# The end of a bidirectional scan kernel: six pairs of units put in another order

## The chip, the cores and the metric

The kernel runs on one core of one Trainium2 chip. A core has a matrix engine (PE, TensorE), whose weight loads are listed apart as PEld, and four others: DVE (VectorE), ACT (ScalarE), POOL (GpSimd) and SP (SyncE), which here only issues DMA transfers. Each engine works through its own list of instructions in order and waits on semaphores for the others. The metric is the device time of one execution in microseconds (us), lower being better.

## The reference

The input is a batch of four images with 128 channels and 96 x 96 points. Each image is normalised in groups, read along rows and along columns, forward and backward (four directions), and each of these sequences goes through a gated convolution and a linear recurrence. The four results are fused by a 1x1 convolution and added to the input. Cut to what matters here:

```python
u, gate = split(grouped_1x1(seq, in_proj))
u  = depthwise_conv5(silu(u))
s, a, bb, cc = ssm_in(u), decay(u), tanh(u @ Wb), tanh(u @ Wc)
hst = scan(a, bb * s)                       # h = a*h + bb*s along the sequence
u  = u + ssm_out(cc * hst + d * s)          # the "state product"
u  = mix(u * sigmoid(gate))
y  = out_proj(u)                            # folded with mix and fuse into one matrix
out = x + sum over four directions of fuse(y)
```

## The kernel before

All weights behind the gate (mix, out_proj, fuse) are folded into one matrix `w_fin`, so what follows the gate is one product. A unit is a quarter (one residue of the position modulo R = 4) of a strip of 16 rows or columns in one direction; it has N = 384 positions. A *pair* is the two units of opposite directions (s = 0 and s = 1) that share the engines' instructions. There are 192 pairs, eight phases (image by orientation) of 24. `pair(t)` starts the front part of a pair and finishes the back part of the pair six earlier (LAG), so when the loop over 192 pairs has ended the back parts of six pairs are left, and `tail()` does them. Nothing but the order in which the lines of `tail()` are written sets the order on each engine: the schedule is by hand, and the semaphores follow from the data.

The back parts in the tail are called here by letters, by the names that the program gives their tiles: A = 7_4_2 and B = 7_4_3 (pairs 186 and 187, the last two of strip 4), and C, D, E, F = 7_5_0 to 7_5_3 (pairs 188 to 191, strip 5, the last of all). Z = 7_4_1 is the pair ahead of them, whose gating is already done when the tail begins. The back part of a pair has these steps:

- *Scan* (L702, DVE): the recurrence over a whole strip, for all its four pairs at once, in two halves. Only C to F still wait for theirs, the last scan of the kernel.
- *Outputs* (L708 and L709, on POOL unless told otherwise): cc times the state, plus the other term, in 64 partitions x 384. A copy (L711 on POOL or, as `z_copy`, L909 on ACT) brings the result to the other 64 partitions.
- *Seed* (`under`, L505, ACT): u of a unit is copied into two PSUM banks, so that the state product adds to it.
- *State product* (`out_of`, L497, PE): four matmuls of 32 partitions into the banks SSM + 2s and SSM + 2s + 1, that is 0 and 1 for s = 0, 2 and 3 for s = 1.
- *Gating* (L577, DVE; for F in halves, L964): (gate + 1) times the PSUM banks, into u.
- *Product* (`accumulate`, L134 under L729, PE): eight matmuls with `w_fin` into one bank of PSUM; one for each unit, called A0, A1, B0 and so on here by pair and s.
- *Addition* into `acc` (L752, L754): for s = 0 through a copy of the bank on ACT (`ys`, L735 or L737) and an addition on POOL, for s = 1 in the tail straight from PSUM on DVE. The last pair's products and additions are in halves of 192 positions (L974 to L991), and each of its four additions releases one output transfer on SP.

`gate_units(n)` (L911) writes, for each s, the gating of pair n and the seed of pair n + 1 in the same banks: the seed has to wait until that gating has read them. `finish(n)` (L919) issues both products of a pair, into the banks 4 and 5 or 6 and 7. `add()` (L924) does the oldest waiting DVE addition and sends finished lines.

In the tail before, the order of the state products, S, and the products on PE is: S(A), Z0, Z1, S(B), A0, A1, B0, B1, S(C), S(D), C0, C1, S(E), D0, D1, S(F), E0, E1, F in four halves. The scan halves lie apart on DVE, with B's gating between them (L934, L937, L938). C's outputs are DVE's and their copy POOL's (L939); those of D, E and F are all POOL's (L940, L943).

Of the kernel before, what the change touches and what calls it, by code (L numbers as in the profile page):

```python
# [45 lines left out]
ALU = mybir.AluOpType  # L46

P = 128
# [19 lines left out]
def conv_preact_kernel(  # L68
# [424 lines left out]

    def out_of(bi, s, j):
        z = tbs[bi]
        r = slice(64 * j + 32 * s, 64 * j + 32 * s + 32)
        nc.tensor.matmul(bank(SSM + 2 * s + j)[:, :N], w_so[r, bass.ts(j, P)], z[r, :],  # L497
                         start=bi not in seeded, stop=True, skip_group_check=True)
# [3 lines left out]
    def under(bi, s):  # L502

        seeded.add(bi)
        nc.scalar.copy(psum[:, SSM + 2 * s : SSM + 2 * s + 2, :N], us[bi][:, s])  # L505
# [60 lines left out]
    def gating(bi, s):  # L566
# [7 lines left out]
        pz = psum[:, SSM + 2 * s : SSM + 2 * s + 2, :N]  # L574
# [131 lines left out]
    def outputs(i, copy=nc.gpsimd.tensor_copy, engine=nc.gpsimd):  # L706
        ta, tb, p = scans[units[i]["step"]], tbs[i], units[i]["p"]
        engine.tensor_mul(ta[0:64, p, :], tb[64:P, :], ta[64:P, p, :])  # L708
        engine.tensor_add(tb[0:64, :], ta[0:64, p, :], tb[0:64, :])  # L709
        if copy:  # L710
            copy(tb[64:P, :], tb[0:64, :])  # L711
# [186 lines left out]
    def tail():  # L898
# [12 lines left out]
        def gate_units(n):  # L911
            for s in range(2):
                gating(2 * n, s)
                under(2 * n + 2, s)
                if s == 0 and n > first + 1:
                    z_copy(n + 1)
            waiting.extend(units[2 * n : 2 * n + 2])

        def finish(n):  # L919
            banks = (4, 5) if n % 2 else (6, 7)  # L920
            accumulate(waiting.pop(0), banks[0])()
            wait.append(accumulate(waiting.pop(0), banks[1], nc.vector, True))

        def add():  # L924
            if wait:
                wait.pop(0)()
# [5 lines left out]
        for bk in (4, 5):  # L932
            accumulate(waiting.pop(0), bk)()
        scan(NU // UB - 1, 0)  # L934
        scale_s(NU - 2)
        ssm_out(first + 1)
        gate_units(first + 1)  # L937
        scan(NU // UB - 1, 1)  # L938
        outputs(2 * first + 4, nc.gpsimd.tensor_copy, nc.vector)  # L939
        outputs(2 * first + 6, None)  # L940
        for bk in (6, 7):
            wait.append(accumulate(waiting.pop(0), bk, nc.vector, True))
        for n in range(first + 4, end):  # L943
            outputs(2 * n, None)
        finish(first + 1)
        add()
        add()
        ssm_out(first + 2)
        for n in range(first + 2, end - 1):
            gate_units(n)  # L950
            add()
            if n > first + 2:
                finish(n - 1)
# [3 lines left out]
        for s in range(2):  # L957
# [3 lines left out]
            for e in range(2):  # L961
                r = bass.ts(e, half)
                pz = psum[:, SSM + 2 * s : SSM + 2 * s + 2, r]
                nc.vector.scalar_tensor_tensor(v[:, :, r], g[:, :, r], 1.0, pz, ALU.add, ALU.mult)  # L964
        add()
        finish(end - 2)
        add()
        for s in range(2):
            bu = units[last + s]
            v = us[last][:, s]  # L970
            for e in range(2):
                r = bass.ts(e, half)
                py = bank(4 + 2 * s + e)
                for j in range(2):  # L974
                    for c in range(4):
                        mm(py, c, w_fin[:, bu["dir"], j, 32 * c : 32 * c + 32], v[:, j, r],
                           j == 0, j == 1)
                y = py[:, :half]
                lines = bu["st"] * LN + e * LN // 2
                if s:  # L980
                    lines = HH - lines - LN // 2
                    y = y[:, ::-1]
                part = acc[:, bass.ds(lines, LN // 2), R - 1 - bu["p"] if s else bu["p"], :]
                y = y.rearrange("p (h m) -> p h m", m=M)
                if s:
                    nc.vector.tensor_add(part, y, part)
                else:
# [190 lines left out]
```

## Time and profile before

Four executions took 1817.16, 1820.51, 1816.78 and 1817.36 us; the median is 1817.26. The profiled execution took 1817.16 us, and the span of its trace, from the first to the last instruction, is 1815.4 us.

| | busy us | share of the span |
|---|---|---|
| PE | 1791.1 | 99% |
| ACT | 1561.7 | 86% |
| DVE | 1446.1 | 80% |
| POOL | 1428.8 | 79% |

The tail takes the last 37 us. From the timeline of that stretch (us from the start of the span):

| step | start |
|---|---|
| S(A) on PE | 1778.65 |
| Z0, Z1 on PE | 1779.68, 1781.37 |
| first half of the last scan on DVE | 1781.55 |
| S(B) on PE | 1782.80 |
| B's gating on DVE | 1783.81 |
| A0, A1, B0, B1 on PE | 1784.18 |
| second half of the last scan on DVE | 1785.67 |
| C's outputs on DVE | 1787.60 |
| S(C) on PE | 1789.57 |
| S(D) on PE | 1793.07 |
| S(E) on PE | 1800.13 |
| S(F) on PE | 1803.70 |
| last product ends on PE | 1810.42 |
| the four last additions end on DVE | 1809.04, 1809.61, 1810.27, 1810.85 |

In the views that follow, the chain of waits gives start, length, what; the timeline adds the operation, the output and input, the count of instructions merged and, in brackets, the idle time ahead and what ended it; the table by stretches gives for each engine the busy time and the number of instructions, then PEclk, the share of full speed that TensorE's clock was granted. PE's rows count two records for each matmul. A busy PE is one with a matmul under way, at whatever clock.

### The profile page before, as it was taken

What the parts mean: (1) busy time and instruction counts of PE and PEld (TensorE: products, weight loads), DVE (VectorE), ACT (ScalarE), POOL (GpSimd) and SP (SyncE); (2) the same over time, 40 slices, a digit from 0 to 9 for tenths busy, and PEclk for the clock granted to TensorE, in tenths of its full rate; (3) what the DMA queues carried; (4) which work ended last, traced back from release to release, by engine and by line L of the source; (5) the groups of instructions that cost most, each with busy time, mean ns of one, the idle gap of its engine ahead of it and who ended that gap; (6) DMA issues with size and microseconds to landing.
All of it is one profiled execution on the core that took longest, in us unless ns stands there. A gap on an engine that the chain in (4) does not pass through costs nothing.

```text
span 1815.4 us, 56931 instructions
## 1 busy us (share of the span) xinstructions
PE 1791.1 (99%) x24074; PEld 645.9 (36%) x24074; DVE 1446.1 (80%) x1462; ACT 1561.7 (86%) x2748; POOL 1428.8 (79%) x1475
## 2 busy tenths in 40 slices
PE   7999999999999999999999999999999999999998
PEld 3333333333333333333333333333333333333333
DVE  6888878787888887877778888787877788778886
ACT  4888888988988888898888888889888888888974
POOL 3587888788778888788877888878877888887785
PEclk9999999999999999999999999999999999999998
DMA  8555463444975465334696456453476643635434
GB/s 247 177 188 180 148 201 102 161 144 156 315 241 183 158 195 174 118 140 138 222 295 227 141 178 211 120 172 116 155 245 217 227 148 129 198 100 180 149 123 157
DMA packets 148047, 321.17 MB, mean 177 GB/s; under 512 B 14160, under 2 KB 115920, under 8 KB 147792
## 3 DMA queue, kind: packets, MB, share of 16 engines
q1 hardware_dynamic: 147648, 317.48, 53.4%
q8 instruction: 190, 3.11, 0.7%
q14 instruction: 65, 0.53, 0.1%
q10 hardware_dynamic: 144, 0.04, 0.0%
HBM read 185.21 MB, written 132.25 MB: 175 GB/s over the span
## 4 chain that ended last, share of the span: by engine, by line
PE 94%; DVE 2%; DMA 2%; ACT 1%; issue 0%; POOL 0%; SPq 0%; DVEq 0%; ACTq 0%; POOLq 0%
PE psum L134 81%; PE psum L497 8%; PE psum L491 5%; DVE psum L630 1%; DMA x_in<-in_xs 1%; DMA xs<-in_xr 1%; DVE u L577 0%; DMA acc<-in_xr 0%; DVE u L630 0%; ACT psum L505 0%; ACT psum L628 0%; ACT sil L470 0%; ACT u L611 0%; DVE t L702 0%; SPq L296 0%
## 5 line engine op out<-in xcount | busy, mean ns | idle before, releaser
L630 DVE SCALAR_TENSOR_TENSOR psum<-sil,small,psum 128x768 f32<-128x768 f32 x576 | 589.0, 1022 | 28.2 <-ACT psum L628 3.4
L577 DVE SCALAR_TENSOR_TENSOR u<-gate,psum 128x768 f32<-128x768 f32 x376 | 349.7, 953 | 273.9 <-ACT u L609 122.3
L134 PE MATMUL psum<-u,w_fin 128*32 128x384 f32 x6176 | 552.1, 487 | 0.2 <-ACT t L673 0.2
L134 PE MATMUL psum<-u,main 128*32 128x384 f32 x6144 | 534.7, 489 | 1.2 <-DVE u L630 1.1
L754 POOL TENSOR_TENSOR acc<-ys,acc 128x384 f32<-128x384 f32 x374 | 410.9, 1120 | 32.8 <-ACT ys L735 10.1
L708 POOL TENSOR_TENSOR t<-t,t 64x384 f32<-64x384 f32 x191 | 236.8, 1240 | 154.3 <-DVE t L702 70.5
L134 PEld LDWEIGHTS psum<-u,w_fin 128*32 128x32 f32 x6176 | 189.5, 110 | 319.7 <-issue 218.3
L134 PEld LDWEIGHTS psum<-u,main 128*32 128x32 f32 x6144 | 182.3, 110 | 324.0 <-issue 196.5
L505 ACT COPY psum<-u 128x768 f32<-128x768 f32 x352 | 276.7, 799 | 22.7 <-DVE u L630 11.3
L134 PE MATMUL psum<-sil,band 128*32 128x384 f32 x3072 | 285.1, 488 | 0.0
L675 POOL TENSOR_SCALAR t<-tm 64x384 f32<-64x384 f32 x191 | 177.2, 927 | 117.3 <-ACT tm L667 98.3
L709 POOL TENSOR_TENSOR t<-t,t 64x384 f32<-64x384 f32 x191 | 247.0, 1293 | 15.0
L497 PE MATMUL psum<-t,main 32*128 32x384 f32 x1536 | 242.2, 515 | 3.3 <-ACT psum L505 2.6
L628 ACT ACTIVATE psum<-sil,small 128x768 f32<-128x768 f32 x191 | 173.2, 907 | 57.9 <-DVE u L577 49.7
L514 ACT ACTIVATE gate<-psum,bnorm 128x384 f32<-128x384 f32 x384 | 191.8, 581 | 27.1 <-PE psum L491 25.5
L676 POOL TENSOR_TENSOR t<-t,tm 64x384 f32<-64x384 f32 x192 | 195.1, 1016 | 15.3
L630 DVE SCALAR_TENSOR_TENSOR u<-sil,small,psum 128x768 f32<-128x768 f32 x192 | 194.9, 1015 | 7.8
L470 ACT ACTIVATE sil<-psum,bnorm 128x385 f32<-128x385 f32 x384 | 191.8, 584 | 4.0 <-PE psum L134 1.8
L134 PE MATMUL psum<-sil,less 64*32 64x384 f32 x3072 | 168.2, 495 | 0.0
L491 PE MATMUL psum<-x_in,wn 32*128 32x384 f32 x768 | 157.5, 527 | 0.4 <-ACT u L609 0.4
L134 PEld LDWEIGHTS psum<-sil,band 128*32 128x32 f32 x3072 | 90.9, 109 | 169.0 <-issue 94.8
L711 POOL COPY t<-t 64x384 f32<-64x384 f32 x188 | 137.0, 729 | 15.5 <-PE psum L134 3.6
(102 smaller groups left out, 1475.4 us busy)
## 6 DMA issues: line engine op xcount, KB each, us to landing
sil<-sil SPq DMA_DIRECT2D x128, 770.0 KB, 6.6
kept<-gate SPq DMA_DIRECT2D x80, 768.0 KB, 3.7
gate<-kept SPq DMA_DIRECT2D x76, 768.0 KB, 4.6
x_in<-in_xs SPq DMA_DIRECT2D x192, 96.2 KB, 2.5
out<-acc SPq DMA_DIRECT2D x48, 384.0 KB, 7.8
acc<-in_xr SPq DMA_DIRECT2D x39, 384.0 KB, 6.5
xs<-in_xr SPq DMA_DIRECT2D x72, 192.0 KB, 5.5
x_in<-in_xs SPq DMA_DIRECT2D x46, 192.5 KB, 3.4
```

The costliest lines, as they stand in the source:

```text
L134: nc.tensor.matmul(o[r, : rhs.shape[-1]], lhsT, rhs, start=start, stop=stop, skip_group_check=True)
L470: nc.scalar.activation(sils[step][:, s, j, g, :], bank(bk)[:, : N + 1], AF.Silu, bias=bn[:, 1:2] if j else bn[:, 4 + g : 5 + g],)
L491: nc.tensor.matmul(bank(to)[:, :N], stats[un["b"]][0][r, s, :], x_in[s][r, q, off : off + N], start=True, stop=True)
L497: nc.tensor.matmul(bank(SSM + 2 * s + j)[:, :N], w_so[r, bass.ts(j, P)], z[r, :], start=bi not in seeded, stop=True, skip_group_check=True)
L505: nc.scalar.copy(psum[:, SSM + 2 * s : SSM + 2 * s + 2, :N], us[bi][:, s])
L514: nc.scalar.activation(gv[:, s, j, :], bank(to[2 * s + j])[:, :N], AF.Tanh, bias=bn[:, 2 + j : 3 + j], scale=0.5,)
L577: nc.vector.scalar_tensor_tensor(v, g, 1.0, pz, ALU.add, ALU.mult)
L630: nc.vector.scalar_tensor_tensor(us[i][:, :, 1, :] if k == K - 1 else part, src, w_tap[:, k : k + 1], part, ALU.mult, ALU.add,)
L676: nc.gpsimd.tensor_mul(ta[0:64, p, :], tb[0:64, :], tm[0:64, :])
L708: engine.tensor_mul(ta[0:64, p, :], tb[64:P, :], ta[64:P, p, :])
L709: engine.tensor_add(tb[0:64, :], ta[0:64, p, :], tb[0:64, :])
L754: adder.tensor_add(part, y, part)
```

## The change

Only what lies behind the last pair is changed, by these edits:

- The last four pairs' state products take their banks in turn, (6, 7), (0, 1), (2, 3), one turn for each half pair: C in 6 and 0, D in 2 and 6, E in 0 and 2, F in 6 and 0 (the first bank of s = 0 and of s = 1). Products lie in banks 4 and 5 alone, one for s = 0 and one for s = 1.
- Both halves of the last scan stand together on DVE, ahead of B's gating. C's outputs are done on POOL in halves of 192 positions, each behind its half of the scan, and ahead of Z's two additions there. C's copy is ACT's `z_copy`.
- D's outputs go from POOL to DVE. POOL's order is C's outputs, Z's additions, E's outputs, the additions of A0 and B0, F's outputs, the additions of C0, D0, E0.
- On PE products and state products alternate: S(A), Z0, Z1, S(B), A0, A1, B0, S(C), B1, C0, S(D), C1, D0, S(E), D1, E0, S(F), then halves: E1, F0, F0, E1, F1, F1.
- `outputs` takes a range of positions, and the loop over the last products takes six halves rather than four, two of them E1's.

```diff
+    turning = (6, 0, 2)
+
+    def ssm(bi, s):
+        k = bi - NU + 8 + s
+        return turning[k % 3] if bi >= NU - 8 else SSM + 2 * s
...
-        nc.tensor.matmul(bank(SSM + 2 * s + j)[:, :N], w_so[r, bass.ts(j, P)], z[r, :],
+        nc.tensor.matmul(bank(ssm(bi, s) + j)[:, :N], w_so[r, bass.ts(j, P)], z[r, :],
...
-    def outputs(i, copy=nc.gpsimd.tensor_copy, engine=nc.gpsimd):
+    def outputs(i, copy=nc.gpsimd.tensor_copy, engine=nc.gpsimd, r=slice(0, N)):
...
             for s in range(2):
                 gating(2 * n, s)
                 under(2 * n + 2, s)
-                if s == 0 and n > first + 1:
-                    z_copy(n + 1)
-            waiting.extend(units[2 * n : 2 * n + 2])
-
-        def finish(n):
-            banks = (4, 5) if n % 2 else (6, 7)
-            accumulate(waiting.pop(0), banks[0])()
-            wait.append(accumulate(waiting.pop(0), banks[1], nc.vector, True))
+
+        def product(n, s, bk):
+            if s == 0:
+                accumulate(units[2 * n], bk)()
+            else:
+                wait.append(accumulate(units[2 * n + 1], bk, nc.vector, True))
...
         gate_units(first)
-        for bk in (4, 5):
-            accumulate(waiting.pop(0), bk)()
-        scan(NU // UB - 1, 0)
+        adds = [accumulate(waiting.pop(0), bk) for bk in (4, 5)]
         scale_s(NU - 2)
+        for part in range(2):
+            scan(NU // UB - 1, part)
+            outputs(2 * first + 4, None, r=bass.ts(part, N // 2))
         ssm_out(first + 1)
+        for held_add in adds:
+            held_add()
         gate_units(first + 1)
-        scan(NU // UB - 1, 1)
-        outputs(2 * first + 4, nc.gpsimd.tensor_copy, nc.vector)
-        outputs(2 * first + 6, None)
-        for bk in (6, 7):
-            wait.append(accumulate(waiting.pop(0), bk, nc.vector, True))
-        for n in range(first + 4, end):
-            outputs(2 * n, None)
-        finish(first + 1)
-        add()
+        outputs(2 * first + 6, None, nc.vector)
+        outputs(2 * first + 8, None)
+        product(first, 0, 4)
+        product(first, 1, 5)
+        z_copy(first + 2)
+        product(first + 1, 0, 4)
+        outputs(2 * first + 10, None)
         add()
         ssm_out(first + 2)
         for n in range(first + 2, end - 1):
             gate_units(n)
+            z_copy(n + 1)
+            product(n - 1, 1, 5)
             add()
-            if n > first + 2:
-                finish(n - 1)
+            product(n, 0, 4)
             ssm_out(n + 1)
...
-        add()
-        finish(end - 2)
-        add()
-        for s in range(2):
-            bu = units[last + s]
...
+        spots = iter((5, 4, 2, 3, 7, 6))
+        for i, s, e in ((-2, 1, 0), (-1, 0, 0), (-1, 0, 1), (-2, 1, 1), (-1, 1, 0), (-1, 1, 1)):
+            i += NU // 2
+            bu = units[2 * i + s]
+            r = bass.ts(e, half)
+            py = bank(next(spots))
+            for j in range(2):
+                for c in range(4):
+                    mm(py, c, w_fin[:, bu["dir"], j, 32 * c : 32 * c + 32], us[2 * i][:, s, j, r],
+                       j == 0, j == 1)
```

## The prediction

> **What bounds the kernel now.** I read the page first: PE is busy for 1791.1 of 1815.4 us and holds 94% of the chain of waits. Up to 1778.65 us both kernels issue the same instructions on every engine, so only the last 37 us can differ. There I read the chain of waits first (start, length, what):
>
> ```profile
> 1789.57 0.38 PE psum L497
> 1789.95 0.46 DVE acc L754
> 1790.41 0.72 issue
> 1791.13 0.97 DVE u L577
> 1792.10 0.02 issue
> 1792.12 0.81 ACT psum L505
> 1792.93 0.14 issue
> 1793.07 2.79 PE psum L497 x6
> 1795.86 4.34 PE psum L134 x32
> 1800.20 0.86 PE psum L497 x8
> 1801.06 2.72 PE psum L134 x32
> ```
>
> Behind S(C) PE has no product left to issue: the chain leaves it for C's gating and for the seed that must wait for that gating, and PE stands for 2.02 us (1791.05 to 1793.07). Then S(D) and two products take 2.79 and 4.34 us; a little later S(E) and two products take 0.86 and 2.72. The same work at two speeds: the table by stretches says why (length, busy us of the engines, then PEclk).
>
> ```profile
> 1791.10:1793.00 1.90, 0.00 (x0) 0.00 (x0) 1.87 (x3) 0.85 (x2) 1.75 (x3) 0.81 0.00 0
> 1794.00:1795.00 1.00, 1.00 (x6) 0.51 (x5) 0.00 (x0) 0.16 (x1) 1.00 (x1) 0.50 0.06 16
> 1798.00:1800.00 2.00, 2.00 (x20) 0.50 (x12) 0.00 (x0) 0.70 (x2) 1.32 (x2) 0.72 0.27 104
> ...
> 1788.87:1792.28 3.41, 2.16 (x20) 0.60 (x8) 2.69 (x5) 0.19 (x2) 2.54 (x3) 1.00 0.03 10
> 51.50:54.91 3.41, 2.73 (x64) 0.96 (x64) 3.34 (x5) 2.57 (x6) 1.30 (x2) 1.00 0.06 15
> 1792.28:1795.69 3.41, 2.62 (x8) 1.47 (x8) 1.64 (x3) 1.85 (x3) 3.18 (x4) 0.50 0.02 5
> 1795.69:1799.10 3.41, 3.41 (x26) 1.10 (x28) 1.32 (x2) 2.40 (x4) 2.86 (x3) 0.50 0.00 0
> ```
>
> The clock falls to 0.50 at 1792.28 (0.81 over the first stretch puts it there) and is back at 1799.10, 6.82 us later; it falls again at about 1812.74 (0.76 over 1812.5 to 1813.0), 13.64 later. Both are multiples of 3.41, so I read it as set at the end of such stretches: 2.16 busy of 3.41 lost the clock, 2.73 kept it, 2.62 did not win it back, 3.41 did.
>
> Third, whether DVE and POOL can work beside each other:
>
> ```profile
> 1748.63 2.81 DVE L702 TENSOR_TENSOR_SCAN t<-t,t 64x768 f32<-64x768 f32 x1
> 1748.63 1.20 POOL L709 TENSOR_TENSOR t<-t,t 64x384 f32<-64x384 f32 x1
> 1749.89 1.85 POOL L711 COPY t<-t 64x384 f32<-64x384 f32 x1
> ...
> 1781.55 1.81 DVE L702 TENSOR_TENSOR_SCAN t<-t,t 64x768 f32<-64x768 f32 x1
> ```
>
> Alone a scan half takes 1.81 us. Beside POOL it takes 2.81: it ends 1.61 after POOL's operation ends, and POOL's next one, a copy of 0.50 elsewhere, takes 1.85, to 0.30 behind the scan. So a DVE operation with two SBUF inputs and a POOL operation take turns. The gating, with one input in PSUM, takes 0.95 each beside POOL.
>
> Last, the end: the four output transfers (384 KB each) move 393 GB/s, about 1.0 us each, but their additions end only 1.81 us apart. So they queue, and the end follows the first of these additions (1809.04), 6.36 us behind it.
>
> **The change, step by step.** Prices: a product 1.35 (four in 5.37), a state product 0.85 to the next product and 1.05 to the first gating (1766.82 to 1767.88), two gatings 0.97 and 1.82, a seed 0.80, a `ys` 0.58, a z_copy 0.51, a half product 0.67 (E's two whole products and F's four halves take 5.39 together).
>
> *Scan halves and C's outputs.* The first half stays at 1781.55 to 1783.36. The second now starts at 1783.39, ends at 1785.22, 2.35 earlier. POOL is released a few hundredths behind DVE's own start (0.08 at 1688.56) and so waits for it. Its half-size operations are in no trace: the nearest rows are 1.20 (64x384) and, from below, 0.11 for POOL's smallest memset; halving the part that grows gives 0.65, bounds 0.55 and 1.20. Four of them, the first partly spent waiting: 1785.22 to 1787.75. Against that, DVE did C's outputs in 1.79 and POOL copied in 0.50 (to 1790.08). So C's result is 2.3 earlier. B's gating moves from 1783.81 to 1785.25; what waits for it is the seed of C's second half (bank 0) at 1786.24 to 1787.04; behind that in ACT's queue stands the ys of A0, to 1787.56, which frees bank 4 for B0. PE, done with A1 at 1786.88, waits 0.72 there: the first price of the order.
>
> *D's outputs on DVE* start at 1787.1, while POOL does C's last half and Z's additions (about 1.0 each). By the turns above: POOL to 1787.75, DVE's multiplication to 1788.50, one addition of Z to 1789.35, DVE's addition to 1790.10; 3.0 for what is 1.79 alone, bounds 1.8 and 4.2. Queued behind on DVE are A1's addition (to 1790.65) and C's gating.
>
> *PE.* B0 1787.60 to 1788.95, S(C) to 1789.80 (its copy is done at 1788.3, both seeds at 1787.04). B1 needs bank 5, free when A1 is added: PE waits 0.90, the second price. B1 1790.70, C0 1792.05 (C's gating 1790.67 to 1791.64), S(D) 1793.40. That is 0.33 later than before. From here each pair is S, product, product with nothing between: ACT has the seeds ready, because the banks turn (the bank of D's second seed, 6, is last read by C's first gating, a whole step earlier), and the z_copy ends 2.8 to 3.3 after S begins, ahead of the next S at 3.55. So S(E) 1796.95, S(F) 1800.50: 3.2 earlier than before. Of the 7.06 between S(D) and S(E), half speed and seed waits were 3.5.
>
> *POOL behind it:* Z's second addition to 1790.95, E's outputs to 1793.4, A0 and B0 added to 1795.4, F's outputs to 1797.8. F's copy is wanted by ACT at 1799.75: 1.95 of cover. B's four output transfers leave SP at about 1795.4, not 1798.65, and are through by 1799.5, before the last four. Halving E1 adds no matmul time (two of 0.67); it fills PE while F is gated.
>
> *The end.* F's gating 1801.55, four times 0.49, to 1803.50; E1's half addition 0.37, then F0's 0.43: first of the last four at 1804.30 against 1809.04. From S(F) that is 3.80 instead of 5.34. PE ends at 1805.4, the last addition at 1805.9, before 1810.85. Sum: 0.33 - 3.51 = -3.2 at S(F), -1.5 behind it, **-4.7 us**. The span becomes 1810.7; with the 1.76 outside the span the profiled execution's 1817.16 becomes 1812.5, and the median, 0.10 above, 1812.6. I say 1812.5.
>
> Bounds: half operations at 1.20 delay C's copy by 2.2, of which 0.65 is covered: +1.6. POOL ahead of the second scan half: +0.65. D's outputs between 1.8 and 4.2: -0.7 to +1.2. Together some 1811.3 to 1814.7, not all at once.
>
> **A rule against the trace.** The row comes first: a stretch of 3.41 us with 2.16 busy, and no idle time above 2.02, lost the clock. The Trainium skill, TensorE: Matmul & The Clock Gate, Part 1, says that the clock halves after at least one idle window of about 3.4 us, and its table warns of gaps above some 3 us. By the page no gap of the changed kernel comes near and the sum stands. By the row, 0.72 + 0.90 of waiting within 3.9 us could leave a stretch as little as 2.2 busy, and the time would be that of the first rival.
>
> **The rivals.** *The clock still falls* at one of the two new waits. For: 2.2 busy at the worst phase against 2.16 that lost it. Against: at the phase of this trace the stretches hold 2.7 and 2.5, near the 2.73 that kept it, and behind 1790.7 PE is continuous, so one or two stretches bring it back. Price: half of 3.41 or 6.82, 1.7 to 3.4: 1814.2 to 1815.9.
>
> *POOL and DVE in turns cost more than I give*: the half operations at their upper bound, or D's outputs losing every turn. For: no row of them. Price 1.0 to 2.5: 1813.5 to 1815.0.
>
> *Slower: the half clock stays.* Place: from 1792.28 on. At half speed S and two products last 7.1; if the state products, 32 partitions deep, count as less than busy, stretches may fall short again and again. It decides from three stretches on (5.1 us lost against 4.7 gained); four cost 6.8: 1819.3. Against: the full stretch 1795.69 to 1799.10 did restore it.
>
> *It does not act as said*: the two scan halves adjacent, yet C's state product hardly moves (0.6), since B0 now stands ahead of it. That is in my sum; if POOL loses fewer turns the gain is 5.5: 1811.8.
>
> **How the numbers follow.** Forecast with its near variants, 1811.5 to 1813.4: 0.60. Clock falls for one or two stretches: 0.20. Costlier turns: 0.11. Half clock stays, slower: 0.09. The range 1810.8 to 1816.0 takes in all but the last and some of the second. About 0.2%, 3.6 us, is what a measurement of this kernel can tell, so faster means below 1813.6: 0.60 and a little of the third, 0.62. Same takes the second and most of the third, 0.29; slower 0.09.
>
> **What would show it.** Right: PEclk 1.00 through to the end; S(D), S(E), S(F) 3.5 apart; waits of PE under 1 us, one before B0 and one before B1; POOL's first half operation stretched to the end of the second scan half; D's two operations on DVE lengthened; first of the last additions near 1804.3. Wrong: any 0.50 before that; a gap ahead of S(F) for F's copy; S(C) later than 1790.5.

## The result, and the profile after

The changed kernel took 1813.69 us (median of 33 executions, 1812.67 to 1817.91) against 1816.60 for the kernel before in the same sessions (53 executions, 1814.69 to 1820.51). The ratio is 0.9985, with a 95% interval of 0.9980 to 0.9990: 2.9 us faster, not 4.7. The profiled execution took 1814.49 us, its span is 1812.7, and the lines of the code are up by 7 (L709 is the scan, L715 and L716 the outputs, L761 the addition, L504 the state product).

The whole kernel is too coarse to see the difference in: S(A), the first step of the tail, stands at 1778.65 in the trace of before and at 1777.27 in that of after, though both kernels issue the same work up to there; in the kernels shown further on it stands between 1778.0 and 1780.3. So stretches that begin at S(A) are compared from here on. From S(A) to the end of the first of the last four additions it was 30.4 us before; the prediction made it 25.65; this trace shows 29.0. PE in this trace, with S(A), B0, B1 and C0 together, and S(F):

```profile
1777.27 1.10 PE L504 MATMUL psum<-t,main 32*128 32x384 f32 x8
...
1786.73 1.50 PE L134 MATMUL psum<-u,w_fin 128*32 128x384 f32 x16 [1.16 <-ACT ys L742]
...
1791.25 4.38 PE L134 MATMUL psum<-u,w_fin 128*32 128x384 f32 x32 [2.16 <-DVE acc L761]
...
1802.75 0.93 PE L504 MATMUL psum<-t,main 32*128 32x384 f32 x8
```

The loss against the prediction lies mostly in one place. The chain of waits (start, length, what) in the part that answers to the chain of before:

```profile
1784.38 1.83 DVE u L584 x2
...
1786.23 2.84 DVE t L715
1789.07 0.02 issue
1789.09 0.04 DVE t L716
...
1789.34 1.31 issue
1790.65 0.55 DVE acc L761
1791.20 0.04 issue
1791.25 4.38 PE psum L134 x32
1795.62 0.91 PE psum L504 x8
1796.53 2.72 PE psum L134 x32
1799.25 0.86 PE psum L504 x8
```

Read it upwards from S(D), the 0.91 at 1795.62. B1 and C0, the 4.38 ahead of it, began only when A1 had been added (0.55), since that frees B1's bank. A1's addition stood on DVE behind D's two outputs, and these took from 1786.23 to 1790.7, the second of them in the piece called "issue": it was under way, and the profile names nothing that it waited for. Also, B1 and C0 took 4.38, while the next two products took 2.72. The table by stretches (length, busy us of PE, PEld, DVE, ACT, POOL with the count, then PEclk, DMA share, GB/s), laid along the grid of 3.41 us on which the clock changes here (it falls at 1792.29 and is back at 1795.70), says why:

```profile
1785.46:1788.88 3.42, 2.26 (x28) 0.73 (x24) 3.39 (x2) 2.31 (x5) 3.26 (x5) 1.00 0.54 217
1788.88:1792.29 3.41, 1.25 (x20) 0.47 (x20) 3.38 (x5) 0.91 (x2) 3.33 (x3) 1.00 0.00 0
1792.29:1795.70 3.41, 3.41 (x28) 0.91 (x20) 1.18 (x2) 1.11 (x2) 3.25 (x4) 0.50 0.37 141
1795.70:1799.11 3.41, 3.41 (x40) 1.13 (x40) 2.29 (x3) 2.59 (x4) 1.50 (x2) 1.00 0.84 325
```

The wait of 1.16 before B0 left a stretch with 2.26 busy, which kept the clock; the longer wait before B1 left one with 1.25, and the clock was halved for the next, though PE was busy in all of it. The full stretch brought it back, once, where the kernel before lost it for 6.82. This is the price of the first rival, at its lower end.

What DVE and POOL did meanwhile, and DVE at the end, from the timeline (start, length, engine, line):

```profile
1782.01 2.34 DVE L709 TENSOR_TENSOR_SCAN t<-t 64x768 f32<-64x768 f32 x1
1782.06 0.69 POOL L715 TENSOR_TENSOR t<-t,t 64x192 f32<-64x192 f32 x1 [2.66 <-DVE t L709]
1782.82 2.02 POOL L716 TENSOR_TENSOR t<-t,t 64x192 f32<-64x192 f32 x1
...
1785.70 0.67 POOL L716 TENSOR_TENSOR t<-t,t 64x192 f32<-64x192 f32 x1
...
1786.23 2.83 DVE L715 TENSOR_TENSOR t<-t,t 64x384 f32<-64x384 f32 x1
1786.34 1.95 POOL L761 TENSOR_TENSOR acc<-ys,acc 128x384 f32<-128x384 f32 x2
...
1788.38 1.74 POOL L715 TENSOR_TENSOR t<-t,t 64x384 f32<-64x384 f32 x1
...
1789.09 1.63 DVE L716 TENSOR_TENSOR t<-t,t 64x384 f32<-64x384 f32 x1
...
1805.61 0.35 DVE L989 TENSOR_TENSOR acc<-psum,acc 128x192 f32<-128x192 f32 x1
1805.87 0.73 DVE L991 SCALAR_TENSOR_TENSOR acc<-psum,b_fin,acc 128x192 f32<-128x192 f32 x2
```

Twice POOL wins. Its first half operation, issued 0.05 behind the second scan half, takes 0.69, the length of an undisturbed one, and the scan half takes 2.34 instead of 1.81. Later DVE issues D's multiplication 0.14 before C's last half operation ends on POOL, and both of Z's additions (1.95 together, which is undisturbed) still pass it; POOL's next operation, E's multiplication, is the first that waits for DVE. What such a multiplication takes undisturbed shows in the kernel before, where DVE did C's outputs while POOL stood idle:

```profile
1787.60 0.90 DVE L708 TENSOR_TENSOR t<-t,t 64x384 f32<-64x384 f32 x1
```

Behind S(D) the trace is as predicted. State products start at 1795.55, 1799.18 and 1802.75, 3.6 apart. The rows at 1805.61 and 1805.87 are E1's first half addition and F0's two: the first of F0's ends some 3.5 us after S(F) begins, and the clock is 1.00 up to the last product.

This trace is not the median execution. Of the executions of the changed kernel whose clock is listed, 24 show a mean granted clock of 1.000 and a median of 1813.4 us, eight show 0.999 and 1814.7, among them the profiled one, and two show 0.998 (1817.1 and 1817.9). A whole stretch of 3.41 us at half clock takes 0.0009 off the mean, so by this record the 24 lost none. Half of a stretch, 1.7 us, on top of the 1.4 that the tail of this trace gained (30.4 to 29.0), makes 3.1, near the 2.9 of the medians. The mean alone doesn't say where a clock was lost, so this is worked out and not shown.

### The profile page after: what moved, and what is told of

It reads as the page before. It is cut to its first block, busy times and chain, and to the rows that moved or that the text cites. A ratio compares the mean times of both kernels' runs of the same rounds, so it can differ in the third digit from the quotient of the medians.

```text
span 1812.7 us, 56969 instructions
## 1 busy us (share of the span) xinstructions
PE 1788.8 (99%) x24090; PEld 645.2 (36%) x24090; DVE 1448.5 (80%) x1462; ACT 1562.6 (86%) x2750; POOL 1431.6 (79%) x1477
## 4 chain that ended last, share of the span: by engine, by line
PE 94%; DVE 3%; ACT 1%; DMA 1%; issue 0%; SPq 0%; POOL 0%; DVEq 0%; ACTq 0%; POOLq 0%
PE psum L134 81%; PE psum L504 8%; PE psum L491 5%; DVE psum L637 1%; DMA xs<-in_xr 1%; DMA acc<-in_xr 0%; DVE u L584 0%; DVE bn L298 0%; DVE u L637 0%; ACT psum L635 0%; ACT psum L512 0%; ACT u L618 0%; ACT sil L470 0%; DVE t L715 0%; DVE t L709 0%
## 5 line engine op out<-in xcount | busy, mean ns | idle before, releaser
L134 PE MATMUL psum<-u,w_fin 128*32 128x384 f32 (+1 forms) x6192 | 552.7, 486 | 3.5 <-DVE acc L761 2.2
L761 POOL TENSOR_TENSOR acc<-ys,acc 128x384 f32<-128x384 f32 x375 | 411.8, 1119 | 28.0 <-ACT ys L744 8.5
L715 POOL TENSOR_TENSOR t<-t,t 64x384 f32<-64x384 f32 (+1 forms) x192 | 237.3, 1236 | 156.7 <-DVE t L709 73.1
L716 POOL TENSOR_TENSOR t<-t,t 64x384 f32<-64x384 f32 (+1 forms) x192 | 248.6, 1295 | 15.1
L504 PE MATMUL psum<-t,main 32*128 32x384 f32 x1536 | 239.4, 513 | 1.3 <-ACT psum L512 0.6
```

Of the source, the lines that this page charges most:

```text
L134: nc.tensor.matmul(o[r, : rhs.shape[-1]], lhsT, rhs, start=start, stop=stop, skip_group_check=True)
L504: nc.tensor.matmul(bank(ssm(bi, s) + j)[:, :N], w_so[r, bass.ts(j, P)], z[r, :], start=bi not in seeded, stop=True, skip_group_check=True)
L715: engine.tensor_mul(ta[0:64, p, r], tb[64:P, r], ta[64:P, p, r])
L716: engine.tensor_add(tb[0:64, r], ta[0:64, p, r], tb[0:64, r])
L761: adder.tensor_add(part, y, part)
```

## The experiments

Ratios are against the kernel before on the same chip in the same session, with a 95% interval; the traces, one of each kernel, are compared from S(A) to S(F), which is 25.05 us before, 25.48 after, and 21.85 in the prediction's sum.

**Is the gain the clock?** The kernel before, with nine matmuls that compute nothing needed, into unused columns, where PE stood for 2.02 us:

```diff
+        def warm(n):
+            for _ in range(n):
+                nc.tensor.matmul(psum[:, 4, 384:512], ident, ident, start=True, stop=True,
+                                 skip_group_check=True)
...
         add()
         add()
         ssm_out(first + 2)
+        warm(9)
```

> The kernel before, with nine 128x128 matmuls on PE between S(C) and S(D), into columns that nothing reads; they only fill the 2.02 us in which PE stood. Theory 1 (most of what the change gains is the clock that the kernel before lost there): PEclk stays 1.00 to the end, S(D) to S(E) falls from 7.06 to about 4.1 us, the kernel is about 2.9 us faster than before (0.9984), as much as the whole change. Rival (the gain comes from the order; the clock is a by-product): S(D) to S(E) falls by no more than 1 us, since DVE and ACT set that stretch, and the ratio is 0.9995 or nearer to 1.

The ratio was 0.9986 [0.9976, 0.9996], 1816.04 us against 1818.90. The timeline of PE (the fillers are at L931):

```profile
1790.17 1.49 PE L497 MATMUL psum<-t,main 32*128 32x384 f32 x8
1791.59 2.27 PE L931 MATMUL psum<-ident 128*128 128x128 f32 x18
1793.80 1.94 PE L497 MATMUL psum<-t,main 32*128 32x384 f32 x8
1795.66 2.79 PE L134 MATMUL psum<-u,w_fin 128*32 128x384 f32 x32
1798.38 0.93 PE L497 MATMUL psum<-t,main 32*128 32x384 f32 x8
```

S(D) to S(E), the first two L497 behind the fillers, is 4.58 us instead of 7.06, C's products take 2.79 instead of 4.41, and from S(A) to S(F) it is 22.70. No wait of the order is removed. The other executions agree: nine of the twelve show a mean clock of 0.999 or 1.000, and of the 23 of the kernel before three do. So keeping the clock alone is worth as much as the whole change turned out to be.

**What is left with the clock kept in both?** The changed kernel with five such matmuls before B0 and nine before B1:

```diff
         z_copy(first + 2)
+        warm(5, 6)
         product(first + 1, 0, 4)
         outputs(2 * first + 10, None)
         add()
         ssm_out(first + 2)
+        warm(9, 4)
         for n in range(first + 2, end - 1):
```

`warm` takes how many and the bank in whose unused columns they are written.

> The changed kernel, with five such matmuls ahead of B0 and nine ahead of B1, in the 1.16 and 2.16 us in which PE stands there. Theory 1 (the clock still falls in a part of the executions, and this costs 1.7 us each time): all executions read a clock of 1.000 in the tail, the median falls by about 0.5 us against the changed kernel (0.9982 against before), and its slower executions go. Rival (the spread of the changed kernel's executions is something else): no difference in median or spread.

The ratio is 0.9981 [0.9971, 0.9991], 1815.45 us against the same 1818.90. From S(A) to S(F) 23.92, and behind S(F) the first addition ends 3.5 later, so 27.4 in all against 28.05 of the kernel before with fillers (22.70 and 5.35): the order by itself gains about 0.6 in these traces, and the ratios, whose intervals overlap, don't contradict that. Against the changed kernel's own 0.9985 the ratio isn't distinguishable either; the traces differ by 1.6, the half of one stretch. That every execution would keep its clock was not borne out: seven of twelve show 1.000, two 0.999 and three 0.996 to 0.998, and where those lost it no trace says.

**Is it D's outputs?** Back to POOL, as before the change:

```diff
-        outputs(2 * first + 6, None, nc.vector)
+        outputs(2 * first + 6, None)
```

> The changed kernel with D's outputs on POOL, behind Z's two additions and ahead of E's outputs, instead of on DVE. Theory 2 (on DVE they lose their turns to POOL: 4.49 us from issue to end where 1.79 is the work, and A1's addition, C's gating and B1 wait behind them): PE's wait of 2.16 us ahead of B1 is gone, the clock does not fall, S(C) to S(D) goes from 7.4 to about 3.6 us, and the kernel is 2.0 to 3.5 us faster than the changed one (about 0.997 against before). Rival (POOL is the bound, which is why D went to DVE): D's copy comes too late, a wait of 1 us or more moves ahead of S(D), S(E) or S(F), and the time is that of the changed kernel or longer.

The ratio is 0.9964 [0.9951, 0.9977], 1812.61 us against 1818.90: 6.3 us faster than the kernel before. PE:

```profile
1788.59 1.50 PE L134 MATMUL psum<-u,w_fin 128*32 128x384 f32 x16 [1.15 <-ACT ys L742]
1790.02 0.93 PE L504 MATMUL psum<-t,main 32*128 32x384 f32 x8
1790.87 2.79 PE L134 MATMUL psum<-u,w_fin 128*32 128x384 f32 x32
1793.59 0.93 PE L504 MATMUL psum<-t,main 32*128 32x384 f32 x8
```

The wait before B0 is the same 1.15, that before B1 is gone, B1 and C0 run at full speed, and from S(A) to S(F) it is 21.62, 3.9 less than in the changed kernel's trace. Of this 2.16 is the wait and 1.6 the half clock that followed it in this execution. By the ratios, 0.9985 and 0.9964 with intervals that don't overlap, though from different sessions, the edit that moved work to DVE cost 3.8: in the order of what the whole change gained. With this version the first of the last additions ends 25.1 behind S(A), against 28.05 in the kernel before with fillers, so without that edit the order brings some 2.9 beyond the clock.

**Or only its place beside Z's additions?** D's outputs stay on DVE, but Z's two additions go behind E's outputs on POOL:

```diff
-        for held_add in adds:
-            held_add()
         gate_units(first + 1)
         outputs(2 * first + 6, None, nc.vector)
         outputs(2 * first + 8, None)
+        for held_add in adds:
+            held_add()
```

> The changed kernel with Z's two additions on POOL behind E's outputs instead of ahead of them; D's outputs stay on DVE. Theory 2a (DVE loses the port for as long as POOL's operations follow one another with no wait on POOL's own result, as Z's two additions do; E's outputs wait for one another and let DVE in): D's outputs take 2.5 to 3.0 us from issue to end instead of 4.49, PE's wait ahead of B1 falls from 2.16 to about 0.5 us, and the kernel is 1.5 to 2.5 us faster than the changed one. Rival 2b (DVE gives way to any POOL operation that is ready): D's outputs still take over 4 us, ended by E's outputs, and the time is unchanged.

The ratio is 0.9966 [0.9955, 0.9978], 1813.34 us. DVE:

```profile
1788.81 0.87 DVE L715 TENSOR_TENSOR t<-t,t 64x384 f32<-64x384 f32 x1
1789.71 1.69 DVE L716 TENSOR_TENSOR t<-t,t 64x384 f32<-64x384 f32 x1
```

The pair takes 2.59 from first to last instead of 4.49, the wait before B1 is 0.26, and S(A) to S(F) is 21.95. The ratio can't be told from that of the version before it. So DVE was not the wrong engine; beside Z's additions was the wrong place.

**What are the scan halves together worth?** On the kernel with D's outputs on POOL, B's gating goes back between the halves:

```diff
-        for part in range(2):
-            scan(NU // UB - 1, part)
-            outputs(2 * first + 4, None, r=bass.ts(part, N // 2))
+        scan(NU // UB - 1, 0)
+        outputs(2 * first + 4, None, r=bass.ts(0, N // 2))
         ssm_out(first + 1)
+        gate_units(first + 1)
+        scan(NU // UB - 1, 1)
+        outputs(2 * first + 4, None, r=bass.ts(1, N // 2))
         for held_add in adds:
             held_add()
-        gate_units(first + 1)
```

> The kernel with D's outputs on POOL, one part of the change undone: B's gating stands again between the scan halves, and Z's two additions stand behind both of C's half outputs as they did. Theory 3 (the adjacent scan halves bring nothing by themselves: what C's result gains, B's gating loses, and B0's bank with it): PE's wait of 1.15 us ahead of B0 falls below 0.3 us and a wait of 1 us or so appears ahead of S(C) instead; the time is within 0.5 us of the kernel with D's outputs on POOL (0.996 to 0.9967 against before). Rival (adjacent halves are worth the 2.35 us by which the second half ends earlier): 1.5 us or more slower than that kernel.

The ratio is 0.9975 [0.9965, 0.9984], 1814.12 us against 1819.18. The wait before B0 is gone, since B's gating and the seed behind it are early; in its place PE waits for C's and D's results on POOL:

```profile
1789.39 1.46 PE L504 MATMUL psum<-t,main 32*128 32x384 f32 x8 [0.80 <-POOL t L716]
1790.79 2.79 PE L134 MATMUL psum<-u,w_fin 128*32 128x384 f32 x32
1793.89 1.46 PE L504 MATMUL psum<-t,main 32*128 32x384 f32 x8 [0.32 <-POOL t L716]
```

S(A) to S(F) is 22.58, 0.96 more than with the halves together: between the two expectations. The halves together bring about 1 us, and that is net of the wait before B0, which they make. This rests on the two traces; the intervals of the ratios, 0.9975 and 0.9964, overlap.

**What are the turning banks worth?** On the same kernel the last pairs' state products stay in banks 0 to 3 (and the last halves take banks that are then free):

```diff
-        return turning[k % 3] if bi >= NU - 8 else SSM + 2 * s
+        return SSM + 2 * s
...
-        spots = iter((5, 4, 2, 3, 7, 6))
+        spots = iter((5, 4, 6, 7, 0, 1))
```

> The kernel with D's outputs on POOL, another part undone: the state products keep their banks 0 to 3, so each seed waits for the gating of its own half, and F's halves use the banks 6, 7, 0, 1. Theory 4 (the turning banks are what lets the next state product follow two products directly): PE waits 0.5 to 0.8 us ahead of S(D), S(E) and S(F), 3.57 us from one to the next become 4.1 to 4.4, and the kernel is 1.5 to 2.4 us slower than with D's outputs on POOL. Rival (two products cover the seeds in either bank): no difference.

The ratio is 0.9994 [0.9985, 1.0003], 1816.92 us: nothing is left that can be told from the kernel before.

```profile
1790.63 1.50 PE L134 MATMUL psum<-u,w_fin 128*32 128x384 f32 x16 [2.02 <-ACT ys L742]
...
1795.63 1.58 PE L504 MATMUL psum<-t,main 32*128 32x384 f32 x8
1797.14 2.79 PE L134 MATMUL psum<-u,w_fin 128*32 128x384 f32 x32
1799.86 1.54 PE L504 MATMUL psum<-t,main 32*128 32x384 f32 x8
```

From S(D) on state products take 1.54 to 1.58 instead of 0.93 and stand 4.2 apart, as the banks of their seeds are read by a gating until shortly before; and the wait before B0 is longer by 0.87. S(A) to S(F) is 23.75, 2.1 more.

This trace also bears on the clock. PE stood for 2.02 us, as long as in the kernel before, and the clock stayed at 1.00. It falls at 1812.73, after the last product; counted back from there in steps of 3.41, the grid puts this row around the wait:

```profile
1788.83:1792.25 3.42, 1.62 (x20) 0.61 (x24) 0.87 (x2) 2.25 (x5) 3.34 (x4) 1.00 0.34 135
```

So 1.62 busy kept the clock here, where 2.16 lost it in the kernel before. Busy time alone is then not what decides. The two differ in what PE did: of the 2.16, 1.48 was a state product, 32 partitions deep, and 0.68 a product; of the 1.62, 0.19 was a state product and the rest a product. Whether a state product counts for less was not tested.

**A faster version.** The seeds of C wait for B's gating, and A0's `ys` stands behind them on ACT; that is the 1.15 before B0. So, on the kernel with D's outputs on POOL, A0's product and its `ys` are issued ahead of B's gating, its addition follows on POOL behind E's outputs, and B0 is added straight from PSUM by DVE:

```diff
-        for held_add in adds:
-            held_add()
+        adds.append(accumulate(units[2 * first], 4))
         gate_units(first + 1)
         outputs(2 * first + 6, None)
+        for held_add in adds[:2]:
+            held_add()
         outputs(2 * first + 8, None)
-        product(first, 0, 4)
+        adds[2]()
+        outputs(2 * first + 10, None)
         product(first, 1, 5)
         z_copy(first + 2)
-        product(first + 1, 0, 4)
-        outputs(2 * first + 10, None)
+        wait.append(accumulate(units[2 * first + 2], 4, nc.vector, True))
+        add()
         add()
```

> The kernel with D's outputs on POOL, and besides: A0's copy out of its bank on ACT goes ahead of C's seeds, B0 is added by DVE straight from PSUM, and POOL does D, Z, E, A0, F in this order. If PE's 1.15 us ahead of B0 are nothing but ACT's order (A0's copy behind a seed that waits for B's gating), they fall below 0.3 us, S(C) begins 0.9 to 1.3 us earlier after S(A), and the kernel is 0.9 to 1.3 us faster than with D's outputs on POOL (0.9955 to 0.996 against before). Rival (POOL's result for C is as late as the bank): the wait moves ahead of S(C), and the gain is under 0.3 us.

PE has no wait between S(B) and S(F), and S(A) to S(F) is 20.46, 1.16 less, as expected. The time was 1811.60 (1809.67 to 1817.96) and the ratio 0.9965 [0.9951, 0.9978], which isn't distinguishable from the version that it was made from; 1 us is within the intervals.

**The last product in halves.** The version with D's outputs on POOL, with E1 whole ahead of F's halves:

```diff
+        product(end - 2, 1, 5)
+        add()
-        spots = iter((5, 4, 2, 3, 7, 6))
-        for i, s, e in ((-2, 1, 0), (-1, 0, 0), (-1, 0, 1), (-2, 1, 1), (-1, 1, 0), (-1, 1, 1)):
+        spots = iter((4, 2, 7, 6))
+        for i, s, e in ((-1, 0, 0), (-1, 0, 1), (-1, 1, 0), (-1, 1, 1)):
```

> The kernel with D's outputs on POOL, but E1's product and addition whole, ahead of F's four halves, in place of two halves among them. The prediction's term: the halves add no matmul time, and what halving brings is DVE's first addition of 0.37 instead of 0.55 ahead of F0's. From the start of S(F) to the end of the first of the last four additions 3.7 us instead of 3.5; the end of the last product and of the last addition within 0.1 of the other kernel's when counted from S(F); the time behind S(F) 0.1 to 0.2 longer. Rival (the halves matter for PE): PE stands idle for F's gating without them, the last product ends 0.4 us or more later from S(F), and the time behind S(F) grows by as much.

It was run once. From S(F) (1799.58) the last product ends after 4.96 us and the last addition after 5.39; with the halves it is 5.15 and 5.56. So two halves of a product do cost PE 0.19 more than a whole, which the prediction put at nothing. The span ends 10.1 us behind S(F) against 10.0: the end follows the first transfer, and that is some 0.2 earlier with the halves. They gain about 0.15, too little for the times to show.

**How do DVE and POOL share?** Four small kernels, each run once, had DVE's pair of output operations beside additions on POOL. The first had four independent, then four chained additions (`work`) in plain tiles; `first` is an addition on POOL that releases DVE:

```python
def dve():
    nc.vector.tensor_mul(z[0:64, :], x[64:P, :], gate[64:P, :])
    nc.vector.tensor_add(y[0:64, :], z[0:64, :], y[0:64, :])
...
for work in (apart, chained):
    first()
    dve()
    work()
```

> A kernel by itself, which computes nothing of the reference: three turns of two DVE operations of the size of D's outputs (64x384, both inputs in SBUF, the second needing the first), released by the end of one POOL addition (128x384) behind which POOL has four more, once each on a tile of its own and once each needing the one before. Theory 2a (POOL keeps the port as long as its next operation is ready at once): beside the four that need nothing, DVE's first operation takes the length of all four, 4 to 5 us, and beside the four that need each other the two engines take turns, some 1.5 to 2.5 us for it. Rival 2b (DVE gives way to any POOL operation): over 4 us in both. Rival 2c (turns are always taken): 1.5 to 2.5 us in both.

Alone the first operation takes 0.55 in these plain tiles, where it took 0.90 in the strided ones of the kernel before. Beside either sort it took 1.33 and the second 1.23: turn about, so this kernel doesn't show what the changed kernel showed. The second kernel took the real strided tiles and let DVE arrive at twelve points of the additions:

> A kernel by itself: it computes nothing of the reference. Twelve turns; in each a POOL addition releases a DVE operation into PSUM whose length grows from turn to turn by some 0.06 us, so that D's two output operations (here in the real strided tiles) arrive at DVE at another point of the four independent POOL additions (in the strided shape of Z's additions) each time. Theory 2d (the point of arrival decides): when DVE's operation arrives in the last 0.15 us or so of a POOL addition it waits through the next one or two as well, 2 to 3 us long, and 1.3 to 1.6 at the other points; over twelve turns one to three are long. Theory 2e (the shapes decide): with these strided views DVE always waits for two additions or more, 2.5 us and up in all twelve turns. Theory 2c (turns are always taken): in all twelve turns the first operation takes between 0.6 and 1.6 us, the rest of the addition under way and its own 0.6, none above 1.7; then what held D's first output operation for 2.83 us stays open.

In the first ten of the twelve turns the first operation took 0.83 to 1.37, less the later it came; in the last two, where it arrived just as the first addition ended (0.02 us before, in the eleventh), it lost one more turn and took 1.67 and 1.60. Never two. The third put on POOL what stood there in the changed kernel, two half operations of which the second waits for the first, two additions, and a whole pair:

> A kernel by itself: it computes nothing of the reference. As the one before, but POOL's operations are those that stood beside D's outputs: a multiplication and an addition of 192 positions, the second waiting for the first, then two independent additions in the shape of Z's, then a whole multiplication and addition like E's. DVE's pair arrives at twelve points, some 0.06 us apart, between about 0.6 us and 1.3 us behind the start of POOL's half operations, so from the middle of the first to the end of the second. Theory 2f (the sequence decides): where DVE arrives late in the second half operation its first operation waits through both additions, 2.5 to 3.0 us, as in the changed kernel; where it arrives earlier it gets in behind the half operation, 0.6 to 1.3. Theory 2c (first come, first served): never above 1.7, as in the sweep before; then what the changed kernel shows comes from something that none of the three small kernels has, and stays open.

This one shows it, in all twelve turns and at every point. The timeline of the second turn, where L92 and L93 are the output operations of both engines and L106 the additions:

```profile
30.12 0.67 POOL L93 TENSOR_TENSOR tb<-t,tb 64x192 f32<-64x192 f32 x1
30.20 3.18 DVE L92 TENSOR_TENSOR t<-tb,t 64x384 f32<-64x384 f32 x1
30.75 1.93 POOL L106 TENSOR_TENSOR acc<-ys,acc 128x384 f32<-128x384 f32 x2
32.76 1.68 POOL L92 TENSOR_TENSOR t<-tb,t 64x384 f32<-64x384 f32 x1
```

DVE's operation lasts to 33.38. In these tiles it takes 0.83 where POOL waits for it (the kernel's first), so it got going at about 32.55, as the second addition was ending (32.68). POOL's next operation, which waits for POOL's own earlier work and so left a gap of 0.08, was the first that waited for DVE: 1.68 instead of 1.19. It took 3.25 in the first turn and 2.54 in the last, and ended at the same place each time. The last kernel varied what stands around the additions. In it `mul_add` is a pair of output operations, the second waiting for the first, what is left out first releases DVE early or late, and what is left out next is two independent half additions:

```python
def turn(late, halves, k, whole):
    ...
    mul_add(nc.vector, 0)
    if halves == 1:
        mul_add(nc.gpsimd, 1, slice(N // 2, N))
    elif halves == 2:
        ...
    additions(k)
    if whole:
        mul_add(nc.gpsimd, 2)
```

> A kernel by itself: it computes nothing of the reference. In the small kernel before, DVE's first operation waited through both additions in all twelve turns, at every point of arrival; with four additions and no half operations it got in behind the first. This one varies what stands on POOL around the additions, each plan with an early and a late arrival: four additions; two and a whole pair; four and a whole pair; halves and four; halves and two; halves, two and a whole pair (the changed kernel's order); two independent half additions, two and a whole pair. Theory 2g (a dependent pair ahead of the additions makes POOL keep its place): DVE waits through both or all four additions, 2.5 us and up, in the plans with the dependent halves and in no other, where it takes 0.7 to 1.7. Theory 2h (DVE gets in only ahead of a POOL operation that waits for POOL's own earlier work): it waits through all the additions in every plan in which they carry no wait, halves or not, so also in two and four with a whole pair behind them in their second turn, and with four independent additions it gets in behind the first, since those wait for the same place of the turn before.

Neither theory fits. Two turns of it, the first with four additions and a whole pair, the other with halves, four additions and nothing else before the next turn's first operation (L101):

```profile
48.61 4.43 POOL L98 TENSOR_TENSOR acc<-ys,acc 128x384 f32<-128x384 f32 x4
...
49.27 2.92 DVE L92 TENSOR_TENSOR t<-tb,t 64x384 f32<-64x384 f32 x1
...
74.80 6.25 DVE L92 TENSOR_TENSOR t<-tb,t 64x384 f32<-64x384 f32 x1
75.09 3.83 POOL L98 TENSOR_TENSOR acc<-ys,acc 128x384 f32<-128x384 f32 x4
78.88 1.46 POOL L101 TENSOR_TENSOR gate<-gate 128x768 f32<-128x768 f32 x1
80.42 1.18 POOL L92 TENSOR_TENSOR t<-tb,t 64x192 f32<-64x192 f32 x1
```

In the first turn, without halves, DVE still waited through three additions and got in ahead of the fourth (4.43 holds one turn of about 0.6; undisturbed they take 3.83). In the second it lost all four and L101 as well, five operations that follow one another without a gap, and got in at the gap of 0.08 behind L101. The longest such operation in this kernel took 8.13 us. With two independent half additions in place of the halves DVE got in behind the next addition (2.11 and 1.70). What the four kernels have in common: where POOL left a gap, DVE got in there if it was waiting; where POOL's operations followed one another without one, DVE got in behind the first, behind the third, or not at all. What decides between these is open.

## Why the prediction was right and wrong

**The direction, the range and the largest term were right.** The time lies in the range, but not among the forecast's near variants, 1811.5 to 1813.4: 1813.69 is where the prediction put its second rival, POOL and DVE in turns at a higher cost (1813.5 to 1815.0), to which it gave 0.11. By its own signs, too, the trace is not the one that it described: the clock is at 0.50 before the end, and both waits of PE are above 1 us. The version with one edit undone comes near the sum, 25.1 us from S(A) to the end of the first of the last additions against 25.65 predicted (29.0 in the changed kernel's trace), though partly because terms cancel: it has no wait before B1 where the sum has 0.90, and 1.15 before B0 where the sum has 0.72.

**The step that failed is D's outputs on DVE.** The sum took 3.0 us, by turns operation by operation, with 4.2 as the upper bound; it was 4.49, above that bound. DVE was to get in behind C's last half operation and then behind one addition of Z; it waited through both. The wait before B1 was 2.16 instead of 0.90.

**With it came the first rival, in the profiled execution.** It had named the condition, a stretch as poorly filled as 2.2, and the price, half of 3.41 or of 6.82; one stretch with 1.25 busy came, and 1.7 was lost. It came at the second wait alone: the stretch with 2.26 busy, around B0, kept the clock. The fall comes at the end of the stretch that holds this wait. That the wait brought it is likely but not shown beyond that: with the waits filled the trace keeps the clock, and so do most executions without fillers. So in this trace two rivals happened at once, the first, as far as the trace tells, as the effect of the second; the prediction had priced them apart. The executions with a mean clock of 1.000, most of them, kept the clock, so what they fell short by is the second rival and the scan halves: the two waits are longer than in the sum by 1.70 together, and the medians gain 1.8 less than the sum. No trace was taken of such an execution, so this is worked out.

**The scan halves.** The second was to end 3.67 us after the first began; it took 4.19, since POOL's half operation got in ahead. This is the bound of +0.65 that the prediction gave, at 0.5, and it passes through B's gating, the seed and the `ys` to the wait before B0: 1.16 for 0.72. That it "does not act as said" was half right. C's state product began 10.9 us after S(A) in both kernels, where the sum had it 0.6 earlier, with one product more behind it instead of ahead. Still, together the halves are worth about 1 us (the experiment), of 2.3 that C's result is earlier.

**The half operations** took 0.67 to 0.71, where 0.65 had been interpolated. The bound of 1.20 wasn't needed.

**The rhythm behind S(D)** was right: S, product, product 3.55 apart predicted, 3.6 measured, and the experiment on the banks shows that the turning banks make it (4.2 without). **The end** was 0.3 better than predicted, 3.5 from S(F) to the first addition instead of 3.80: neighbouring operations of DVE overlap by about 0.1 in the trace, which the sum had end to end. That the halves of E1 cost no matmul time was wrong by 0.19, hidden behind the transfers.

**The clock's share.** The prediction gave 3.5 of its 4.7 to half speed and seed waits between S(D) and S(E). The fillers in the kernel before bear out that most of what the change gained is the clock: 0.9986 without any reordering, and S(D) to S(E) shorter by 2.5 of the 3.5.

**The rule on the clock.** The Trainium skill, TensorE: Matmul & The Clock Gate, Part 1, has the clock halve after at least one idle window of about 3.4 us. Read as a gap in PE's work, this would have cost nothing in either kernel; here the longest idle time of PE was 2.16 us and the clock was halved. The measurement decides. But the prediction's reading, that the busy time in a stretch decides, doesn't hold for all traces either: 1.25 busy of 3.41 lost the clock here and 2.16 in the kernel before, 2.26 kept it here, and 1.62 kept it with the banks fixed. Products alone would separate them, 1.04 and 0.68 us in the stretches that lost it against 1.5 to 1.6 in the last two that kept it; and the 2.62 that did not win it back in the kernel before were state products alone. This fits what the prediction supposed under its slower rival, that state products count as less than busy, and is not tested.

**The rule on the shared port.** The Trainium skill, SBUF — State Buffer, 🔬 SBUF: two separate sides, calls the port pair of DVE and GpSimd an exclusive lock that whoever starts first holds for the whole instruction. The row of POOL's half operation at 1782.06, undisturbed while the scan half waits, agrees with a lock held for an instruction, though not with the order: DVE had issued 0.05 earlier. And Z's second addition, issued more than 1 us after DVE's multiplication, went first, which a lock for one instruction doesn't explain. Here the rows decide.

## What to carry to other kernels

An operation moved to another engine to balance the load is priced by what runs beside it on a shared port, and by what stands behind it in its queue: here 4.5 us for 1.8 of work, and the bank that PE needed stood behind it. Where a matrix engine has a short gap, look at what it does in each stretch of the clock's grid and not only at how long the gap is: 2.02 us lost the clock in one of these traces and not in another. A handful of matmuls that compute nothing can be worth as much as a new order, and they tell at once how much of a loss is the clock. Before a trace is taken for the kernel, see whether the other executions show its clock: here most did not lose what the profiled one lost. When a reordering of several edits gains less than its sum, undo them one at a time: one of them can be eating what the others bring.

## What the runs showed of the hardware that was not expected

- DVE can lose several turns in a row: 2.83 us for an operation of 0.90 in the changed kernel, 2.54 to 3.25 in twelve of twelve turns of the small kernel with the same order, 8.13 at most (0.83 where POOL waits). In these runs it got in wherever POOL left a gap of 0.07 to 0.09 between two operations, and only sometimes where it left none.
- POOL's operation can pass a DVE operation that was issued 0.05 us earlier (2.34 us for a scan half of 1.81).
- The clock does not follow the length of a gap, nor PE's busy time alone: 2.16 busy of 3.41 lost it in one trace, 2.26 and 1.62 kept it in two others. PE being busy in the whole next stretch didn't bring it back before that stretch's end.
- Two products over 192 positions took 0.19 us more than one over 384, in the one pair of traces that compares them.
